# A graph layer's score rows: transposed on TensorE for each block, or stored in DRAM and fetched broadcast

## The chip, the cores and the metric

The kernel runs on one core of a Trainium2 chip. The metric is the device time of one execution in microseconds (us); less is better. Three executions of the kernel before took 2270.28, 2272.42 and 2273.19 us; the median, 2272.42, is the time before. The profile is of one execution more.

## The reference, cut to what matters

Two graph layers run over the same 3327 nodes. Layer 0 adds a normalised neighbour sum and a top-p attention, two steps each, to the features (256 wide). Layer 1, where the change lies, is graph attention with 4 heads of 64 features:

```python
h  = relu(layernorm(x))
hp = (h @ W).reshape(n, 4, 64)
s, d = einsum(hp, a_src), einsum(hp, a_dst)          # one score per head and node
e  = leaky_relu(s[:, :, None] + d[:, None, :], 0.2)  # head, row i, neighbour j
e  = where(adj > 0, e, -inf)
attn = softmax(e, axis=2)
x  = x + elu(einsum('hij,jhf->ihf', attn, hp))
```

The kernel uses that exp(leaky_relu(s+d)) is the larger of exp(s+d) and exp(0.2(s+d)). Up to a factor that belongs to row i alone, and so cancels in the softmax, that is qd[j] = exp(d[j]) times the larger of exp(0.8 s[i]) and low[j] = exp(-0.8 d[j]). The exp(0.8 s[i]) of a block's rows i, for each head, standing equal in all 128 partitions, are what the kernel calls both. A partition is a neighbour j.

## The kernel before

The nodes are padded to NP = 3328 = 26 tiles of 128. `fast` builds a list of some thousand pieces with `plan.put`: an engine, an estimated length, a rank, what must be done before (needs), and named buffers taken and given back. `Plan.order` (L497) plays this list against the estimated times, each engine taking the ready piece of the lowest rank, and the instructions are issued in that order. Nothing is reordered later: each engine works through its own queue, and the DMAs of nearly all pieces stand in the queue of SP. So a change of the list can also move pieces that it doesn't name.

Layer 0 (its second step is the stage before layer 1) works row tile by row tile. For a tile, TensorE makes 128 x 3327 logits (L845, from qq and kt), ScalarE their exponentials and counts (L856, L893, the latter writing to a scratch tile junk), VectorE the search for the top-p threshold and the cut (L948 to L1003), TensorE turns the kept weights (L1016, ScalarE copying, L1021) and multiplies them by the features (L1028). Beside it, `full` multiplies the adjacency by the features: L1049 loads up to four 128 x 128 tiles into one of four buffers at, L1060 multiplies, with the buffer c as the moving operand in step 1, L1067 and L1082 take the sum away. `finish2` (L1251) then does the tile's LayerNorms, its projection (L1289, L1298) and writes the tile's scores: sd (L1308, s and d of four heads), qd and low (L1303, L1304), and hp times qd into main (L1309).

Layer 1 is `attend_neighbours` (L1440). It has four blocks b of W = 832 output rows. Each block goes over the 26 neighbour tiles j:

- SP loads the block's adjacency for tile j into two at buffers (L1513); ScalarE makes a mask of 0 and 1 from it, in bfloat16 in a buffer et (L1523, L1524, two parts each).
- VectorE makes 4 x 832 exponents (L1535): larger of both and low, times mask. They go to one of four buffers e, or, for two tiles in six, to the two halves of rhs, which are free after layer 0 ("e2").
- TensorE multiplies them by main (L1551, into the two PSUM tiles pl) and, after each third tile, by qd for the denominators of three tiles (L1565, acca and accf).

At a block's end ScalarE copies the sums out of PSUM into one e buffer (L1605, L1608), TensorE turns them (L1626), VectorE inverts (L1630), ScalarE does the ELU's two functions (L1638), VectorE adds (L1642, L1643), and SP stores (L1646).

The row factors both are made by `broadcast` (L1463). For each of the 7 tiles that a block touches, four transposes of a score column spread over 128 columns (L1473) leave the row in all partitions in PSUM, and ScalarE's exponential (L1477) writes it into a half of the buffer c; the halves alternate between blocks. They need the tile's scores and `opened` (L1460): c is in use until all neighbour sums of layer 0 are added. Block b+1's pieces have a rank in the middle of block b, and need the end of block b-1, which used the same half.

Of the kernel before, what the change touches and what calls it, by code (L numbers as in the profile page):

```python
# [10 lines left out]
F32 = mybir.dt.float32  # L11
# [559 lines left out]
def fast(  # L571
# [33 lines left out]
    sd = const.tile([P, 2, NT, H], F32, name="sd")  # L605
    qd = const.tile([P, NT, H], F32, name="qd")
    low = const.tile([P, NT, H], F32, name="low")

    far = const.tile([P, 2], F32, name="far")
    bad = const.tile([P, STEPS, NT], F32, name="bad")  # L610
# [15 lines left out]
    with ExitStack() as l0:  # L626
# [184 lines left out]
            a = plan.put("ACT", 0.6, rank, exps, needs=[a])  # L811
            return plan.put("DVE", 0.6, rank, rest, needs=[a])

        plan = Plan(dict(pl=2, px=2, acca=1, accf=1, accf0=1, accf1=1, et=3, at=4, y=1, e2=2, mask=2, **BUFS))

        class Row:

# [532 lines left out]
        def search(row, rank, keys, stats_of, fresh):  # L1350
# [26 lines left out]
                ]  # L1377
                a = plan.put("POOL", (3.8, 4.7)[j], rank - (2.0, 1.6)[j], row.step, j, GP, needs=[got, more])
            if EVALS[n] == 3:
                a = plan.put("ACT", 3.05, rank - 1.4, row.count, 2, AF.Sign, needs=[a])  # L1380
                a = plan.put("DVE", 2.7, rank - 1.3, row.step, 2, V, needs=[a])
            halves = []
            for h in range(2):
# [56 lines left out]
        def attend_neighbours(rows, ends, done, fulls):  # L1440
# [2 lines left out]
            W = NP // 4  # L1443
            C = W // 2
            JG = 3
            logits_done = rows[-1].pieces["logits"]
            freed = [p for p in done]
            extra = {}

# [2 lines left out]
                return [both_of[:, k * NP : (k + 1) * NP].rearrange("p (h w) -> p h w", h=H) for k in range(2)]  # L1452

            def open_heads():
                extra["both"] = halves_of("c", None)

            def open_more():
                extra["e"] = halves_of("rhs", None)

            opened = plan.put("SP", 0.02, 59.0, open_heads, needs=[fulls], lag=0.0)  # L1460
            more = plan.put("SP", 0.02, 59.0, open_more, needs=[freed], lag=0.0)

            def broadcast(b, rank):  # L1463

                lo, hi = b * W, (b + 1) * W
                got = []
                for t in range(lo // P, -(-hi // P)):
                    held = {}

                    def turn(t=t, held=held):  # L1470
                        held["pb"] = ps_x.tile([P, H, P], F32, name="px")
                        for k in range(H):
                            T.transpose(held["pb"][:, k, :], sd[:, 0, t, k : k + 1].to_broadcast([P, P]), ident)  # L1473

                    def exps(t=t, held=held):
                        x0, x1 = max(lo, t * P), min(hi, t * P + P)
                        S.activation(  # L1477
                            extra["both"][b % 2][:, :, x0 - lo : x1 - lo],
                            held["pb"][:, :, x0 - t * P : x1 - t * P],
                            AF.Exp,  # L1480
                            scale=1.0 - ALPHA,
                        )

                    a = plan.put("PE", 0.55, rank, turn, needs=[ends[t][0], opened, used_heads[b % 2]], take=["px"])
                    got.append(plan.put("ACT", 0.65, rank, exps, needs=[a], give=["px"]))
                return got

            used_heads = [None, None]
# [2 lines left out]
            for b in range(4):  # L1491
# [14 lines left out]
                for j in range(NT):  # L1506
                    rank = r0 + 9.0 * j / NT
                    held = {}

                    def load(g, j=j, held=held, tiles=tiles):  # L1510
                        ts = tiles[4 * g : 4 * g + 4]
                        at = held[g] = apool.tile([P, 4, P], F32, name="at")
                        nc.sync.dma_start(  # L1513
                            at[:, : len(ts), :], adjt[ts[0] : ts[0] + len(ts), :, j, :].rearrange("i p q -> p i q")
                        )
# [9 lines left out]

                    def exponents(a, j=j, held=held, b=b):
                        if a == 0:
                            k = j % 6
                            held["e"] = (
                                epool.tile([P, NP], F32, name="e").rearrange("p (h w) -> p h w", h=H)  # L1530
                                if k < 4
                                else extra["e"][k - 4]
                            )
                        for k in (2 * a, 2 * a + 1):
                            V.scalar_tensor_tensor(  # L1535
                                held["e"][:, k, :],
                                extra["both"][b % 2][:, k, :],
                                low[:, j, k : k + 1],
                                held["mask"],
                                ALU.max,  # L1540
                                ALU.mult,
                            )
# [16 lines left out]
                    def sums(j=j, held=held, q=q, open_den=open_den):  # L1559
# [11 lines left out]
                                    tile_position=(0, 32 * k),  # L1571
                                )

                    loads = [
                        plan.put("SP", 0.1, rank, load, g, needs=[logits_done], take=["at"], lag=4.0) for g in range(2)
                    ]
                    m_ = plan.put("ACT", 2.2, rank, mask, needs=[loads], take=["et", "mask"], give=["at", "at"])
                    mine = "e" if j % 6 < 4 else "e2"
                    x_ = plan.put(
                        "DVE", 2.1, rank, exponents, 0, needs=[m_, both, ends[j][0], more if mine == "e2" else None,  # L1580
                        logits_done, last_e], take=[mine], hold=2.0,
                    )
                    y_ = plan.put("DVE", 2.1, rank, exponents, 1, needs=[x_], give=["et", "mask"], hold=2.0)
                    last_e = y_
                    x_ = plan.put(
                        "PE", 1.42, rank, product, 0, needs=[x_, last_acc, evacuated], take=["pl", "pl"] * (j == 0)
# [196 lines left out]
```

## Time and profile before

| What | Value |
|---|---|
| median of three executions | 2272.42 us |
| the profiled execution: time; span of its trace | 2271.77; 2269.9 us |
| ScalarE, GpSimd busy | 1480.0 (65%), 915.3 us (40%) |
| products L1551 into pl, from e and from rhs | 1664 matmuls of 128 x 416 |
| exponents L1535 | 416 of 128 x 832 |
| row exponentials L1477 | 28, median 590 ns |
| mask operations L1523, L1524 | 208 each, 112.1 and 114.5 us |
| loads at, 256 KB | 416, 2.7 us to landing in the median |
| HBM read over the span | 157.66 MB |

Each float32 matmul of the code appears as two in the profile, each transpose as one. PE is TensorE's matmul stream, PEld its weight loads, DVE VectorE, ACT ScalarE, POOL GpSimd, SP the engine whose queue issues the DMAs (SPq). The time of one record includes its way through the engine; what an engine gets through per time is seen from the distance of the starts. The profile's waits name who released an engine last. Layer 1 takes from about 1757 us to the end of the span, 2269.9.

### The profile page before, as it was taken

Reading aid. Unit: us, or ns where it says so; the run is one execution under the profiler, and the core shown is the slowest. Engines: PE = TensorE matmul, PEld = TensorE weight load, DVE = VectorE, ACT = ScalarE, POOL = GpSimd, SP = SyncE. Lnnn points to the kernel's source line nnn. Section 1 sums busy time; section 2 is a strip of 40 time slices with the busy share of each in tenths; the row PEclk is TensorE's granted clock in tenths of the full one; section 3 lists DMA queues with packets and bytes.
Section 4 is the critical chain, followed back from the end, with each engine's and each line's share of the span. In section 5 each row is a group of like instructions: output and inputs, shape, how many; then the busy total and the mean of one; then the engine's idle time right before and its main releaser. Section 6 shows DMA issues by size and latency. Waiting matters only on the chain. (4 is left out here: it accounts for less than half of the span.)

```text
span 2269.9 us, 36125 instructions
## 1 busy us (share of the span) xinstructions
PE 2207.6 (97%) x11956; PEld 1547.5 (68%) x11956; DVE 1618.2 (71%) x4273; ACT 1480.0 (65%) x2849; POOL 915.3 (40%) x2263
## 2 busy tenths in 40 slices
PE   7999999999999999999999999999999999999997
PEld 5477778777877778877878777878788433343332
DVE  5576656557565562277878898678776898989895
ACT  5766686677666851478887877777872646565553
POOL 6455555546533540256646656665561000000000
PEclk9999999999999999999999999999999999999998
DMA  3011221212212222531222122222222443434341
GB/s 98 20 37 53 83 69 53 64 51 61 74 48 74 69 82 76 183 86 54 65 57 73 56 61 70 70 75 75 67 74 78 119 118 107 120 106 120 102 126 42
DMA packets 189653, 176.96 MB, mean 78 GB/s; under 512 B 14866, under 2 KB 145808, under 8 KB 189328
## 3 DMA queue, kind: packets, MB, share of 16 engines
q1 hardware_dynamic: 187472, 173.30, 26.3%
q8 instruction: 96, 1.57, 0.3%
q10 hardware_dynamic: 1984, 1.26, 0.2%
q14 instruction: 101, 0.83, 0.1%
HBM read 157.66 MB, written 15.89 MB: 76 GB/s over the span
## 5 line engine op out<-in xcount | busy, mean ns | idle before, releaser
L1028 PE MATMUL acca<-rhs,et 128*128 128x256 f32 x2704 | 621.2, 380 | 0.8 <-ACT et L1021 0.8
L893 ACT ACTIVATE junk<-e,sc 128x3327 fp8e5<-128x3327 f32 x182 | 559.1, 3072 | 59.1 <-POOL sc L938 57.8
L1028 PEld LDWEIGHTS acca<-rhs,et 128*128 128x128 f32 x2704 | 498.5, 190 | 63.8 <-ACT et L1021 2.6
L1060 PE MATMUL accf<-main,at 128*128 128x257 f32 x1352 | 314.0, 382 | 4.9 <-DMA at<-in_adjt_dram 4.6
L1060 PE MATMUL accf<-c,at 128*128 128x256 f32 x1352 | 313.4, 382 | 4.8 <-ACT f L1067 4.7
L1535 DVE SCALAR_TENSOR_TENSOR e<-c,low,et 128x832 f32<-128x832 f32 x288 | 289.0, 1076 | 16.3 <-ACT e L1605 9.7
L1060 PEld LDWEIGHTS accf<-c,at 128*128 128x128 f32 x1352 | 250.2, 190 | 54.8 <-issue 14.1
L1060 PEld LDWEIGHTS accf<-main,at 128*128 128x128 f32 x1352 | 250.7, 191 | 47.1 <-issue 8.2
L1021 ACT COPY et<-px 128x512 f32<-128x512 f32 (+1 forms) x364 | 193.6, 553 | 133.3 <-PE acca L1028 72.5
L948 DVE SCALAR_TENSOR_TENSOR y<-e,sc 128x1664 f32<-128x1664 f32 x104 | 206.6, 1987 | 96.3 <-POOL sc L935 63.8
L953 DVE MAX8 cands<-y 128x8 f32<-128x208 f32 x832 | 242.7, 361 | 3.7
L1003 DVE SCALAR_TENSOR_TENSOR e<-e,thr 128x832 f32<-128x832 f32 x208 | 212.6, 1080 | 1.7
L1551 PE MATMUL pl<-e,main 128*64 128x416 f32 x1152 | 212.0, 516 | 0.1
L856 ACT ACTIVATE e<-pl 128x1024 f32<-128x1024 f32 x208 | 179.1, 863 | 45.6 <-PE pl L845 45.3
L1016 PE MATMUL px<-ident,e 128*128 128x128 f32 x1352 | 193.5, 275 | 7.6 <-ACT et L1021 4.5
L1524 ACT ACTIVATE et<-at 128x512 bf16<-128x512 f32 (+1 forms) x208 | 114.5, 550 | 127.6 <-DVE e L1535 82.4
L1016 PEld LDWEIGHTS px<-ident,e 128*128 128x128 f32 x1352 | 160.4, 141 | 51.6 <-issue 12.5
L845 PE MATMUL pl<-kt,qq 64*128 64x512 f32 (+1 forms) x728 | 184.1, 588 | 0.1
L1551 PEld LDWEIGHTS pl<-e,main 128*64 128x64 f32 x1152 | 79.8, 137 | 122.2 <-issue 102.2
L1535 DVE SCALAR_TENSOR_TENSOR rhs<-c,low,et 128x832 f32<-128x832 f32 x128 | 129.2, 1073 | 0.0
L845 PEld LDWEIGHTS pl<-kt,qq 64*128 64x128 f32 x728 | 70.9, 185 | 82.3 <-issue 76.5
L1523 ACT ACTIVATE at<-at 128x512 f32<-128x512 f32 (+1 forms) x208 | 112.1, 539 | 4.3 <-DMA at<-in_adjt_dram 4.2
(486 smaller groups left out, 2834.3 us busy)
## 6 DMA issues: line engine op xcount, KB each, us to landing
at<-in_adjt_dram SPq DMA_DIRECT2D x416, 256.0 KB, 2.7
at<-in_adjt_dram SPq DMA_DIRECT2D x104, 192.0 KB, 3.0
at<-in_adjt_dram SPq DMA_DIRECT2D x52, 128.0 KB, 2.1
ys<-ystage SPq DMA_DIRECT2D x26, 256.0 KB, 2.2
rhs<-in_x_dram SPq DMA_DIRECT2D x26, 128.0 KB, 2.9
ystage<-in_x_dram SPq DMA_DIRECT2D x26, 128.0 KB, 2.0
base<-ys SPq DMA_DIRECT2D x26, 128.0 KB, 2.2
x1s<-ystage SPq DMA_DIRECT2D x26, 128.0 KB, 1.7
```

The costliest lines, as they stand in the source:

```text
L845: T.matmul(pl[:, r, :m], qq[half, self.i, :], kt[half, 512 * k : 512 * k + m], start=True, stop=True,)
L856: S.activation(self.e[:, 1024 * k : 1024 * k + pl.shape[1]], pl, AF.Exp, accum_out=(self.p0, self.p1, self.p2, self.p3)[k],)
L893: S.activation(junk[:, :N], self.e[:, :N], fn, bias=t, scale=-1.0, accum_out=dst, saturate=False)
L948: V.scalar_tensor_tensor(self.y[:, : hi - lo], self.e[:, lo:hi], self.up, self.e[:, lo:hi], ALU.is_lt, ALU.mult, accum_out=(self.h0, self. ...
L953: V.max(self.cands[:, o // PIECE, :], self.y[:, o - lo : min(o + PIECE, hi) - lo])
L1003: V.scalar_tensor_tensor(piece, piece, self.thr[:, o : o + 1], piece, ALU.is_gt, ALU.mult)
L1016: T.transpose(pt[:, k, :], self.e[:, j * P : (j + 1) * P], ident)
L1021: S.copy(self.et[g][:, :m, :], self.pt.pop(g)[:, :m, :])
L1028: T.matmul(self.acc, et[:, j - 4 * g, :], rhs[self.n][:, j, :], start=(j == 0), stop=(j == NT - 1))
L1060: T.matmul(self.acc[:, : self.w], self.at[j // JC][:, j % JC, :], self.src[:, j, : self.w], start=(j == 0), stop=(j == NT - 1),)
L1535: V.scalar_tensor_tensor(held["e"][:, k, :], extra["both"][b % 2][:, k, :], low[:, j, k : k + 1], held["mask"], ALU.max, ALU.mult,)
L1551: T.matmul(q["acc"][a][k * FH : (k + 1) * FH, c, :C], main[:, j, h * FH : (h + 1) * FH], held["e"][:, h, c * C : (c + 1) * C], start=(j == 0),
```

## The change

- **Score rows.** `spread_heads` replaces the transposes of `broadcast`. In four groups of tiles (0 to 6, 7 to 12, 13 to 19, 20 to 25) one transpose turns a group's scores of four heads (up to 28 columns) into rows, one exponential takes them to SBUF (at most 28 partitions x 128), and SP stores them tile by tile, 4 rows of 512 bytes, into `highs`, 4 x 3328 in DRAM. A group's pieces are ready as soon as its scores are; the rank is 30 plus its last tile, at most 59.
- **Broadcast.** `broadcast` is two DMAs for a block, two heads each: 2 x 832 values read for each of the 128 partitions. They need the groups stored, the buffer opened, and the block before the last ended. A block's first half of exponents needs the first DMA, its second half the second.
- **Buffers.** Blocks 0 and 2 have both in the space of qq, free when the logits of the last row are done; blocks 1 and 3 in the first half of c. The second half of c becomes a third "e2", so seven buffers take exponents in turn instead of six.
- **First two tiles.** In block 0, tiles 0 and 1 get their adjacency into the space of kt and their masks into that of junk, by loads and masks of their own (one Relu and one Sign over 832 columns); the other tiles load as before.

```diff
-        logits_done = rows[-1].pieces["logits"]
+        logits_done = [r.pieces["logits"] for r in rows]
...
             def open_heads():
-                extra["both"] = halves_of("c", None)
+                both = wpool.tile([P, NT, P], F32, name="qq").rearrange("p t d -> p (t d)")
+                extra["both"] = [both.rearrange("p (h w) -> p h w", h=H)]
+
+                extra["at"] = wpool.tile([P, 2 * W], F32, name="kt").rearrange("p (k w) -> p k w", k=2)
+                extra["m"] = scr.tile([P, NP // 2], BF16, name="junk").rearrange("p (k w) -> p k w", k=2)
+
+            def open_heads2():
+                both, e = halves_of("c", None)
+                extra["both"].append(both)
+                extra["e"] = [e]
 
             def open_more():
-                extra["e"] = halves_of("rhs", None)
+                extra["e"] += halves_of("rhs", None)
...
+                def turn():
+                    held["ps"] = ps_x.tile([(t1 - t0) * H, P], F32, name="px")
+                    T.transpose(held["ps"], sd[:, 0, t0:t1, :].rearrange("p t h -> p (t h)"), ident)
+
+                def exps():
+                    held["rows"] = small.tile([7 * H, P], F32, name="rows", bufs=1)[: (t1 - t0) * H]
+                    S.activation(held["rows"], held["ps"], AF.Exp, scale=1.0 - ALPHA)
+
+                def store():
+                    for t in range(t0, t1):
+                        nc.sync.dma_start(
+                            highs[:, t * P : (t + 1) * P], held["rows"][(t - t0) * H : (t - t0 + 1) * H, :]
+                        )
...
+            cuts = (0, 7, 13, 20, NT)
+            spread = [spread_heads(*cuts[k : k + 2]) for k in range(4)]
...
                 lo, hi = b * W, (b + 1) * W
-                got = []
-                for t in range(lo // P, -(-hi // P)):
...
-                        for k in range(H):
-                            T.transpose(held["pb"][:, k, :], sd[:, 0, t, k : k + 1].to_broadcast([P, P]), ident)
...
-                    a = plan.put("PE", 0.55, rank, turn, needs=[ends[t][0], opened, used_heads[b % 2]], take=["px"])
-                    got.append(plan.put("ACT", 0.65, rank, exps, needs=[a], give=["px"]))
+                got, after = [], [spread[: b + 1], opened[b % 2], used_heads[b % 2]]
+                for a in range(2):
+
+                    def fetch(a=a):
+                        nc.sync.dma_start(
+                            extra["both"][b % 2][:, 2 * a : 2 * a + 2, :],
+                            highs[2 * a : 2 * a + 2, lo:hi].partition_broadcast(P),
                         )
 
+                    got.append(plan.put("SP", 0.1, rank, fetch, needs=[after], lag=7.0 + 5.0 * a))
                 return got
...
+                    def load_first(j=j):
+                        for t0, t1, w in ((0, W // P, P), (W // P, W // P + 1, W % P)):
+                            nc.sync.dma_start(
+                                extra["at"][:, j, t0 * P : (t1 - 1) * P + w].rearrange("p (i q) -> p i q", q=w),
+                                adjt[t0:t1, :, j, :w].rearrange("i p q -> p i q"),
+                            )
+
+                    def mask_first(j=j, held=held):
+                        held["mask"] = extra["m"][:, j, :]
+                        S.activation(extra["at"][:, j, :], extra["at"][:, j, :], AF.Relu)
+                        S.activation(held["mask"], extra["at"][:, j, :], AF.Sign)
...
-                            k = j % 6
+                            k = j % 7
...
+                    own = ["et", "mask"]
+                    if b == 0 and j < 2:
+                        loads, own = plan.put("SP", 0.2, rank, load_first, needs=[opened[0]], lag=4.0), []
+                        m_ = plan.put("ACT", 1.8, rank, mask_first, needs=[loads])
```

## The prediction

> **What bounds the kernel now.** I read the shares of the page first, then the windows of the last stage, then the chain of waits, then the groups of the lines that the change touches.
>
> ```profile
> PE 2207.6 (97%) x11956; PEld 1547.5 (68%) x11956; DVE 1618.2 (71%) x4273; ACT 1480.0 (65%) x2849; POOL 915.3 (40%) x2263
> ...
> L1535 DVE SCALAR_TENSOR_TENSOR e<-c,low,et 128x832 f32<-128x832 f32 x288 | 289.0, 1076 | 16.3 <-ACT e L1605 9.7
> ```
>
> TensorE is busy for 97% of the span. A busy share alone proves little there, so I look at its pace in layer 1 (chain of waits: start, length, what):
>
> ```profile
> 1787.51 8.53 PE pl L1551 x48
> 1800.36 8.53 PE pl L1551 x48
> 1813.22 8.53 PE pl L1551 x48
> ```
>
> The x48 products of three neighbour tiles start every 12.86 us, so a tile takes 4.286 us on TensorE (products and the denominator sums of L1565), without a gap. VectorE's four exponents of a tile take 4 x 1.003 us (289.0/288) = 4.01 us: 0.28 us per tile less. TensorE is the bound of a steady block, VectorE close behind. The windows cut layer 1 at the last neighbour product of layer 0 (1757.0), the first product of tile 3 (1787.4), the three block borders and the last sum:
>
> ```profile
> 1757.00:1787.40 30.40, 25.18 (x159) 13.45 (x157) 22.60 (x33) 23.31 (x49) 1.85 (x5) 0.89 0.44 125
> 1787.40:1887.10 99.70, 99.70 (x748) 37.71 (x744) 94.78 (x99) 45.51 (x92) 0.00 (x0) 1.00 0.37 107
> 1887.10:2008.50 121.40, 121.19 (x882) 46.61 (x881) 110.06 (x126) 69.66 (x172) 0.00 (x0) 1.00 0.39 114
> 2008.50:2128.70 120.20, 120.20 (x875) 46.21 (x874) 109.24 (x125) 68.77 (x170) 0.00 (x0) 1.00 0.40 115
> 2128.70:2247.70 119.00, 118.41 (x857) 43.92 (x853) 101.91 (x117) 61.01 (x154) 0.00 (x0) 1.00 0.33 96
> ```
>
> Columns: stretch, length, busy PE, PEld, DVE, ACT, POOL, granted clock, DMA share, GB/s. The first stretch is the only one with idle TensorE and a lowered clock: the ramp. Its timeline shows why:
>
> ```profile
> 1760.23 1.50 PE L1473 MATMUL px<-ident,sd 128*128 128x128 f32 x8 [2.15 <-ACT c L1477]
> ...
> 1769.48 16.02 DVE L1535 SCALAR_TENSOR_TENSOR e<-c,low,et 128x832 f32<-128x832 f32 x16
> ...
> 1771.47 1.74 PE L1551 MATMUL pl<-e,main 128*64 128x416 f32 x8
> ```
>
> The score rows of block 0 can be made only after layer 0 has left the buffer c, so the first exponents start 12.5 us after TensorE's last work of layer 0, and TensorE meanwhile transposes rows and waits for ScalarE's copies. The transposes themselves (minimum, median, maximum ns; first and last start):
>
> ```profile
> L1473 PEld LDWEIGHTS px<-ident,sd x112: 133/137/231, 1756.8 to 2081.1; 128*128 128x128 f32 x112
> L1473 PE MATMUL px<-ident,sd x112: 272/273/473, 1757.0 to 2081.3; 128*128 128x128 f32 x112
> ```
>
> Eight in a row (1886.11 to 1887.13) take 1.02 us, so one costs the stream about 0.137 us, its weight load, and not the 273 ns of its record.
>
> **What the Trainium skill says.** (1) "Perfetto Trace Analysis", Identifying the Most-Contended Engine: matmul busy share is no good measure; find the gaps. Here the 12.86 us spacing is that check. (2) "TensorE: Matmul & The Clock Gate", Part 2: only weight loads move ahead, matmuls stay in program order. So a product that waits for VectorE holds all behind it; the trace shows nothing against this. (3) "DMA: Bandwidth & Descriptors", Queues, rings and completion order: SP's DMAs share one ring on each of 16 engines, consumed in order. The trace agrees. Around the 1472 KB load at 814.7 us (issues from 812 to 826: size, us to landing) the neighbour tiles land in 7.9 us, against 2.7 over the run:
>
> ```profile
> qq<-qqs SPq DMA_DIRECT2D x1, 1472.0 KB, 9.5
> at<-in_adjt_dram SPq DMA_DIRECT2D x3, 256.0 KB, 7.9
> ```
>
> (4) Same page, Rules for kernel authors: a DMA that reads what another wrote must wait for the first one's completion before it is issued. The new fetches so wait on SP's queue, in order with the neighbour loads.
>
> **The change, part by part.** For the order I use the instructions of the changed kernel as built.
>
> *Transposes removed.* 112 x 0.137 = 15.3 us of TensorE. Of these 56 lie in the ramp (7.7 us) and 56 in blocks 0 to 2, where nothing covers them. Added: 4 transposes of a whole group of tiles, 0.14 each (same row) = 0.6. Net -14.7.
>
> *Ramp.* The 30.4 us hold 12.9 for three tiles, 2.1 for the last row's transposes and projection, 7.7 for the 56 transposes, and 7.7 of waiting. In the changed order the first product follows the last neighbour product directly: the exponents of tiles 0 and 1 are made before, since block 0's rows come into qq and two masks into kt and junk, all free once the last row is searched. Let that end be T. Tiles 0 and 1 keep TensorE until T+5.7. ScalarE masks tile 2 after the last copy (T+0.4+2.2), VectorE gives its halves at T+4.7 and T+6.7, in time; then the sums to T+12.9. Tile 3 is ready at T+10.7, tile 4 at T+14.7, then the last row's LayerNorm (1.6) and tile 5 at T+20.4, where TensorE waits 0.6. Below that I can't go. Above: block 1's rows, two DMAs of 832 KB, are issued into c at about T+1, as soon as VectorE has read c, and the loads of tile 4 stand behind them in the ring. The step-1 keys (384, 352 and 1472 KB, landed 10.9 us after 813.3) give 207 GB/s, hence an estimate of 8.2 us; at the 300 GB/s that the DMA table reaches in single slices, 5.7. Tile 4 then lands at T+10 to 12, is masked at T+13 to 14, and costs 2 to 4 us. Waiting left: 0.5 to 8 (all of today's), I take 2.5: -5.2.
>
> *Blocks.* A block is 26 x 4.286 = 111.4, plus 21 output transposes (0.80 for the first six, 0.48 for each three, from the timeline: 3.2). With 28 and 20 row transposes (3.8, 2.7) blocks 1 and 2 leave 2.9 and 2.8 us of waiting, block 3 4.4: 10.2 in all, at the borders. Who VectorE waited for there (1880 to 1920: total, times, longest):
>
> ```profile
> DVE e L1535 <- PE accf L1565: 5.5, 2, 4.9
> ```
>
> It sat 4.9 us without a free e buffer and then ran behind. A seventh e buffer lets it go one tile (4.0 us) further, and ScalarE loses 28 exponentials of 0.59. Against this, blocks 2's and 3's fetches are issued at a border, when VectorE ends the block before; behind them stand loads from tile 3 on and the output stores whose buffers ScalarE waits for. Loaded and masked tiles last VectorE about 12 us, against 8.2 plus 2.7 plus a mask of 2.2. I take 8.5 left (bounds 4 and 14): -1.7.
>
> *End of layer 0.* The first six exponents (6.0 us) stand inside row 25's search and row 24's end on VectorE, two masks (estimate 1.8 each from the 512 and 320 wide ones) before rows' copies on ScalarE. Behind them are row 25's transposes, but 40 neighbour products (40 x 0.445, from 12 in 5.34 us, = 17.8) stand ahead of those on TensorE and cover it; before, 18 of them stood at the very end. If that cover fails TensorE waits by the rest. Also 26 stores of 512-byte rows enter SP's queue, about 0.43 us each (kq spreads), up to seven together before neighbour loads: 3.0 us, against four tiles loaded ahead, 7.1 us of products. A store waits for its exponential on ScalarE, and SP with it. The rest of step 1 is only reordered. I take +1.0 (bounds -1 and +4).
>
> *Free edits.* The whole-tile masks save 0.4 us of ScalarE twice, under TensorE's stream; the failing-over test moves only in order.
>
> Sum: -14.7 - 5.2 - 1.7 + 1.0 = -20.6 us. The profiled execution took 2271.77 (span 2269.9 and 1.87 around it), giving 2251.2; it lies 0.65 below the median of the runs, 2272.42, so 2251.5 stands for the median after.
>
> **The rivals.** A: as above, 2251.5, own range 2247 to 2256: 0.50. B: VectorE's extra buffer also ends most border waits (4 left), the ramp waits 0.5 and layer 0 ends unmoved: -14.7 - 7.2 - 6.2 = -28, so 2244: 0.20. For it: the 4.9 us wait for a buffer; against: elu work still sits in ScalarE's queue there. C: the c fetch and the early exponents eat the ramp's gain (0, and +4 at the end of layer 0; borders as now): -10.7, so 2262: 0.19. E: C with 5 to 10 us more lost, for instance SP held by stores in several rows of layer 0: no difference, 2270: 0.05. D, slower: 128 partitions read the same 3.3 KB rows, and if such a read runs at 60 GB/s the 1.7 MB take 28 us; each of three late fetches then outlasts the 12 us of tiles in hand by 16: +48 - 22, 2298: 0.06. It decides from about 85 GB/s (20 us per fetch). Against it: four loads at 227.0 to 228.5, of which 512 KB are broadcast, landed by 234.3 beside neighbour tiles, 768 KB in 7.3 us.
>
> **Numbers.** The range 2243 to 2263 takes A, B's middle and most of C. A measurement of this kernel tells about 0.2% (4.5 us) from no change; faster by more: A, B, C = 0.89; within: 0.05; slower: 0.06.
>
> **What would show it.** L1473 and L1477 gone, PE in layer 1 keeping 12.86 us per three tiles, no PE idle or clock drop after the last L1060, blocks 1 to 3 of 116 to 119 us. Wrong: SP's fetches landing after more than 10 us with neighbour tiles behind them, products ended by VectorE in tiles 4 to 8, or L1060 products waiting for loads in step 1.

## The result, and the profile after

The changed kernel takes 2257.81 us (median of four executions, 2255.93 to 2259.07) against 2271.69 us for the kernel before on the same chip: the ratio is 0.9938, with a 95% interval of 0.9921 to 0.9955. So it is 13.9 us faster. The forecast was 20.6 us faster, 2251.5, with a range of 2243 to 2263. The direction and the range hold, but the time lies outside the prediction's own range for its main case (2247 to 2256), and a third of the forecast gain did not come. The profiled execution took 2258.68 us, its span is 2256.9, 13.0 less than the span before.

I read the same views as for the kernel before. All lines of the code after the change lie lower in the file: L1535 is now L1575 (exponents), L1551 is L1591 (products), L1565 is L1605 (sums), L1060 is L1061 (neighbour sums), L1605 is L1651 (sums to an e buffer), L1626 is L1672 (output transposes), L1630 is L1676 (reciprocals). First the shares of the page and the groups of the exponents, which now come from qq or c:

```profile
PE 2196.9 (97%) x11848; PEld 1535.3 (68%) x11848; DVE 1617.5 (72%) x4273; ACT 1466.3 (65%) x2821; POOL 924.8 (41%) x2263
...
L1575 DVE SCALAR_TENSOR_TENSOR e<-c,low,et 128x832 f32<-128x832 f32 x128 | 128.6, 1075 | 8.0 <-PE accf L1605 4.8
...
L1575 DVE SCALAR_TENSOR_TENSOR e<-qq,low,et 128x832 f32<-128x832 f32 x120 | 120.4, 1076 | 2.6 <-ACT e L1651 2.0
```

TensorE has 108 instructions less (112 transposes out, 4 in), ScalarE 28 less, and TensorE's share is 97% as before. The share does not tell which stage gained. The chain of waits shows the pace of a steady block, x48 products again every 12.86 us:

```profile
1910.91 8.53 PE pl L1591 x48
...
1923.77 8.53 PE pl L1591 x48
...
1936.63 8.53 PE pl L1591 x48
```

The windows of layer 1 (columns as before: length, busy PE, PEld, DVE, ACT, POOL, granted clock, DMA share, GB/s), cut at the last neighbour product, tile 3 and the block borders:

```profile
1760.90:1773.70 12.80, 12.80 (x98) 4.76 (x98) 9.90 (x13) 6.33 (x13) 2.23 (x2) 1.00 0.77 243
1773.70:1877.50 103.80, 102.62 (x749) 38.17 (x745) 100.02 (x111) 53.70 (x110) 3.73 (x3) 1.00 0.46 133
1877.50:1996.70 119.20, 118.00 (x859) 43.82 (x855) 110.21 (x126) 64.72 (x162) 0.00 (x0) 1.00 0.45 130
1996.70:2115.50 118.80, 118.21 (x857) 44.09 (x853) 109.79 (x126) 66.22 (x164) 0.00 (x0) 1.00 0.40 116
2115.50:2234.40 118.90, 118.31 (x858) 44.13 (x854) 100.61 (x116) 60.29 (x152) 0.00 (x0) 1.00 0.33 97
```

The first stretch, 30.4 us with an idle TensorE and a clock of 0.89 before, is 12.8 us without idle time at full clock. The three later blocks are only a little shorter. The starts of the products in the two traces give the whole account (us; "tile 6" is where the third group of three tiles starts):

| Piece | before | after | change |
|---|---|---|---|
| start to the last neighbour product | 1757.21 | 1760.89 | +3.68 |
| from there to tile 6 of block 0 (the ramp) | 43.08 | 28.65 | -14.43 |
| tiles 6 to 23 of block 0 | 77.14 | 79.27 | +2.13 |
| tiles 24 and 25 of block 0 | 9.69 | 8.67 | -1.02 |
| block 1 | 121.39 | 119.18 | -2.21 |
| block 2 | 120.18 | 118.86 | -1.32 |
| block 3 | 119.10 | 118.93 | -0.17 |
| after the last sum | 22.09 | 22.44 | +0.35 |
| sum | | | -12.99 |

The 2.13 us are the last row's own transposes and projection, which stood in the ramp before, and the fourth group's transpose. So the ramp gives 12.3 us, close to the 12.9 of the forecast. The blocks give 4.7 (tiles 24 and 25 of block 0, and blocks 1 to 3) where 9.4 were forecast, and layer 0 ends 3.7 us later where 1.4 were forecast (1.0 and three transposes).

**Where the blocks' gain went.** From the border to tile 6, blocks 1 to 3 take 33.25, 33.05 and 33.22 us before and 33.37, 33.04 and 33.05 after. Twelve transposes stood in this piece of each of blocks 1 and 2 before; they are gone, a buffer has come, and no piece moved by more than 0.2 us. The timeline of TensorE in block 2, the kernel before:

```profile
2008.52 4.41 PE L1551 MATMUL pl<-e,main 128*64 128x416 f32 x24
...
2031.61 0.65 PE L1473 MATMUL px<-ident,sd 128*128 128x128 f32 x4
...
2034.46 1.09 PE L1473 MATMUL px<-ident,sd 128*128 128x128 f32 x8
...
2041.57 7.20 PE L1551 MATMUL pl<-e,main 128*64 128x416 f32 x40
```

and after:

```profile
1996.65 1.62 PE L1591 MATMUL pl<-e,main 128*64 128x416 f32 x8
...
2015.46 2.29 PE L1591 MATMUL pl<-c,main 128*64 128x416 f32 x8
...
2020.05 2.61 PE L1591 MATMUL pl<-rhs,main 128*64 128x416 f32 x8 [0.24 <-DVE rhs L1575]
2022.84 2.61 PE L1591 MATMUL pl<-rhs,main 128*64 128x416 f32 x8 [0.18 <-DVE rhs L1575]
...
2029.70 3.01 PE L1591 MATMUL pl<-rhs,main 128*64 128x416 f32 x16
```

Both reach tile 6 after 33.05 us. After the change, eight products of tiles 4 and 5 take 2.29 and 2.61 us where eight take 1.4 to 1.6 elsewhere: TensorE waits for VectorE between these products, and the merged lines hide the waits. VectorE's own timeline of the changed kernel, at the same border, tells why (brackets: idle before, and who ended it):

```profile
1985.39 8.06 DVE L1575 SCALAR_TENSOR_TENSOR e<-qq,low,et 128x832 f32<-128x832 f32 x8
1995.45 4.07 DVE L1575 SCALAR_TENSOR_TENSOR e<-qq,low,et 128x832 f32<-128x832 f32 x4 [2.01 <-ACT e L1651]
...
2003.08 0.43 DVE L1688 SCALAR_TENSOR_TENSOR ystage<-ystage 128x256 f32<-128x256 f32 x1 [3.39 <-ACT ystage L1684]
...
2006.73 0.18 DVE L1676 RECIPROCAL mv<-px 128x4 f32<-128x4 f32 x1 [2.77 <-PE px L1672]
...
2008.29 2.08 DVE L1575 SCALAR_TENSOR_TENSOR e<-qq,low,et 128x832 f32<-128x832 f32 x2 [0.60 <-PE accf L1605]
```

Tiles 0, 1 and 2 of the block are done at 1999.4; the exponents of tile 3 start at 2008.29, 8.9 us later and 11.64 us after the border. The idle time is put down to three names, but what the exponents themselves wait for is the last one, `PE accf L1605`, the sums of tile 0. Tiles 0 to 3 of every block take the four buffers e, one of which holds the finished block's output at this time, so tile 3 needs the buffer of tile 0, and its sums stand behind the products of three tiles. The buffers for tiles 4, 5 and 6 lie free all the while. In the kernel before it is the same: tile 3 starts again 11.64 us after the border, which lies at 2008.52:

```profile
2020.16 2.08 DVE L1535 SCALAR_TENSOR_TENSOR e<-c,low,et 128x832 f32<-128x832 f32 x2 [0.60 <-PE accf L1565]
```

### The profile page after: what moved, and what is told of

The parts are those of the page before. It is cut to its first block, busy times and chain, and to the rows that moved or that the text cites. A ratio compares the mean times of both kernels' runs of the same rounds, so it can differ in the third digit from the quotient of the medians.

```text
span 2256.9 us, 35921 instructions
## 1 busy us (share of the span) xinstructions
PE 2196.9 (97%) x11848; PEld 1535.3 (68%) x11848; DVE 1617.5 (72%) x4273; ACT 1466.3 (65%) x2821; POOL 924.8 (41%) x2263
## 3 DMA queue, kind: packets, MB, share of 16 engines
q10 hardware_dynamic: 1984, 1.26, 0.2%
## 5 line engine op out<-in xcount | busy, mean ns | idle before, releaser
L1061 PE MATMUL accf<-main,at 128*128 128x257 f32 x1352 | 315.0, 383 | 4.3 <-DMA at<-in_adjt_dram 4.0
L1061 PE MATMUL accf<-c,at 128*128 128x256 f32 x1352 | 313.5, 382 | 5.1 <-ACT f L1068 4.5
L1061 PEld LDWEIGHTS accf<-c,at 128*128 128x128 f32 x1352 | 250.2, 190 | 55.2 <-issue 13.7
L1061 PEld LDWEIGHTS accf<-main,at 128*128 128x128 f32 x1352 | 251.2, 191 | 46.6 <-issue 8.2
L1022 ACT COPY et<-px 128x512 f32<-128x512 f32 (+1 forms) x364 | 193.5, 553 | 134.0 <-PE acca L1029 70.6
L1564 ACT ACTIVATE et<-at 128x448 bf16<-128x448 f32 (+1 forms) x204 | 112.2, 550 | 134.6 <-DVE e L1575 81.0
L1017 PEld LDWEIGHTS px<-ident,e 128*128 128x128 f32 x1352 | 160.2, 141 | 53.6 <-issue 12.8
L1591 PE MATMUL pl<-e,main 128*64 128x416 f32 x1024 | 187.0, 515 | 0.0
L1591 PEld LDWEIGHTS pl<-e,main 128*64 128x64 f32 x1024 | 71.2, 137 | 107.8 <-issue 93.4
L1575 DVE SCALAR_TENSOR_TENSOR e<-c,low,et 128x832 f32<-128x832 f32 x128 | 128.6, 1075 | 8.0 <-PE accf L1605 4.8
L1575 DVE SCALAR_TENSOR_TENSOR e<-qq,low,et 128x832 f32<-128x832 f32 x120 | 120.4, 1076 | 2.6 <-ACT e L1651 2.0
L1563 ACT ACTIVATE at<-at 128x448 f32<-128x448 f32 (+1 forms) x204 | 109.8, 538 | 18.2 <-DMA at<-in_adjt_dram 17.9
```

What stands on the lines that cost most here:

```text
L1017: T.transpose(pt[:, k, :], self.e[:, j * P : (j + 1) * P], ident)
L1022: S.copy(self.et[g][:, :m, :], self.pt.pop(g)[:, :m, :])
L1061: T.matmul(self.acc[:, : self.w], self.at[j // JC][:, j % JC, :], self.src[:, j, : self.w], start=(j == 0), stop=(j == NT - 1),)
L1575: V.scalar_tensor_tensor(held["e"][:, k, :], extra["both"][b % 2][:, k, :], low[:, j, k : k + 1], held["mask"], ALU.max, ALU.mult,)
L1591: T.matmul(q["acc"][a][k * FH : (k + 1) * FH, c, :C], main[:, j, h * FH : (h + 1) * FH], held["e"][:, h, c * C : (c + 1) * C], start=(j == 0),
```

## The experiments

All twelve kernels derive from the changed kernel. "Below before" is the kernel's median under that of the kernel before on the same chip (2272.5 to 2273.4 us there); the changed kernel has 13.9. The pieces are those of the table above.

| Kernel | median us | below before | ratio, 95% interval | border to tile 6, blocks 1, 2, 3 |
|---|---|---|---|---|
| rows turned on TensorE again | 2272.32 | 1.1 | 0.9995, 0.9987 to 1.0003 | 33.84, 33.74, 33.60 |
| six buffers | 2258.31 | 15.1 | 0.9934, 0.9920 to 0.9947 | 33.21, 33.21, 33.22 |
| no own buffers for tiles 0, 1 | 2265.61 | 7.8 | 0.9964, 0.9951 to 0.9978 | 33.60, 33.04, 33.04 |
| turned order of buffers | 2254.97 | 18.5 | 0.9917, 0.9904 to 0.9931 | 29.47, 29.61, 29.61 |
| transposes at the border | 2258.17 | 14.3 | 0.9935, 0.9922 to 0.9949 | 33.51, 33.04, 33.04 |
| transposes in the block | 2264.11 | 8.4 | 0.9962, 0.9948 to 0.9975 | 33.37, 33.60, 33.60 |
| late fetch | 2255.57 | 16.9 | 0.9924, 0.9911 to 0.9938 | 33.37, 33.05, 33.05 |
| rhs first | 2246.50 | 26.0 | 0.9885, 0.9870 to 0.9900 | 29.47, 29.61, 29.61 |
| rhs first and late fetch | 2244.27 | 28.5 | 0.9878, 0.9861 to 0.9894 | 29.47, 29.61, 29.61 |
| the same, rows late | 2250.49 | 22.3 | 0.9903, 0.9886 to 0.9919 | 29.47, 29.61, 29.61 |
| fetches twice | 2258.51 | 14.0 | 0.9940, 0.9926 to 0.9953 | 33.37, 33.04, 33.04 |
| rhs first, late fetch, fetches twice | 2244.62 | 27.9 | 0.9878, 0.9863 to 0.9893 | 29.47, 29.61, 29.61 |

**1. The rows turned on TensorE again.**

```diff
-                        nc.sync.dma_start(
-                            extra["both"][b % 2][:, 2 * a : 2 * a + 2, :],
-                            highs[2 * a : 2 * a + 2, lo:hi].partition_broadcast(P),
-                        )
...
+                        for k in range(H):
+                            T.transpose(held["pb"][:, k, :], sd[:, 0, t, k : k + 1].to_broadcast([P, P]), ident)
```

> The changed kernel, but with its row factors turned on TensorE again (112 transposes and 28 exponentials, no DRAM rows, no fetches); the seven buffers, the space of qq for blocks 0 and 2 and the first two tiles' own buffers stay. Theory: at each of the two inner borders 12 transposes lie in the first six tiles, where TensorE waits for VectorE anyway, so 24 x 0.137 = 3.3 us of the 14.7 were never to be had, and the kernel comes out 8.5 to 11.5 us above the changed one (the fetch of block 1 in front of tile 4's loads also goes, worth up to 3): 2266 to 2269. Rival, the prediction's step (nothing covers the transposes in the blocks): the full 14.7, 2272.5. In the profile the theory expects six tiles after a border to take 33.0 to 33.4 us as in both kernels; the rival 34.7.

Measured: 2272.32, 1.1 us below the kernel before on the same chip, so 12.8 above the changed one. The theory's number missed. The rival's number, 2272.5, was met, but by luck: its six tiles of 34.7 us did not come. Blocks 1 to 3 take 122.14, 121.74 and 119.48 us, 6.4 more than in the changed kernel, of which only 1.7 lie ahead of tile 6; and block 3, which has no transposes, has a third of these (33.60 us instead of 33.05). The rest of the 12.8 I had not foreseen: the early start is gone too. TensorE's timeline at the end of layer 0:

```profile
1748.08 7.93 PE L1061 MATMUL accf<-c,at 128*128 128x256 f32 x36
1755.85 1.04 PE L1510 MATMUL px<-ident,sd 128*128 128x128 f32 x8
...
1768.67 1.62 PE L1602 MATMUL pl<-e,main 128*64 128x416 f32 x8
```

The turns of block 0 stand in TensorE's queue behind the last 36 neighbour products, and the first product follows 12.65 us after the last of these, against 14.27 in the kernel before and none in the changed one. With the buffers alone the change is worth nothing that these runs can tell. SP's queue was what let block 0's rows overtake TensorE's work.

**2. Six buffers.**

```diff
-                            k = j % 7
+                            k = j % 6
...
-                    mine = "e" if j % 7 < 4 else "e2"
+                    mine = "e" if j % 6 < 4 else "e2"
```

> The changed kernel with six exponent buffers in turn as before (the second half of c unused). Theory: the seventh buffer bought nothing at the borders, because tile 3 of a block always waits for a buffer e that the sums of the block's tile 0 free: blocks 1 to 3 stay at 118.9 to 119.2 us each within 0.5, and only the ramp may lose up to 3 us, since tile 4 now needs a half of rhs: 2257.8 to 2261. Rival, the prediction's step (one buffer lets VectorE go a tile, 4.0 us, further at a border): blocks 1 to 3 become 2 to 4 us longer each, 2264 to 2270.

Measured: 2258.31, blocks of 119.03, 119.02 and 119.10 us against 119.18, 118.86 and 118.93, and the ramp's second group of three tiles 16.2 us against 15.9. The theory holds: the seventh buffer bought nothing at a border.

**3. No own buffers for the first two tiles.**

```diff
-                    if b == 0 and j < 2:
+                    if False:
```

> The changed kernel without the first two tiles' own buffers: their loads and masks use the common buffers at and et, rows still through DRAM. Theory: the loads then compete with layer 0's last neighbour loads and the masks with its last turned weights, so the first product comes 3 to 8 us after the last neighbour product instead of at once: 2261 to 2266. Rival (block 0's rows in qq alone make the early start): within 1 us of the changed kernel, 2257 to 2259.

Measured: 2265.61, 6.1 us less gain than the changed kernel. VectorE gets to the first exponents only after the last row's work, and TensorE shows the gap:

```profile
1766.40 13.37 PE L1591 MATMUL pl<-e,main 128*64 128x416 f32 x48 [6.06 <-DVE e L1575]
```

So the early start needs both parts: rows that come by DMA, and places for two tiles' masks. This kernel also answers a question on layer 0, taken up below.

**4. Another order of the same buffers.**

```diff
-                            k = j % 7
+                            k = (j + (0, 5, 4, 4)[b]) % 7
```

The line that names the buffer taken (`mine`) changes in the same way, here and in run 8.

> The changed kernel with the same seven buffers taken in another order: blocks 1 to 3 begin with the halves of rhs and c, free by then, instead of with the four e, of which a block's output takes one. Theory: VectorE's idle time at a border (2.0 us before tile 2, 8.9 before tile 3) goes, TensorE's waiting of 4.2 to 4.5 us per border falls to 0.5 to 1.5, blocks 1 to 3 take 115.5 to 116.5 us and the kernel 2247 to 2250. Rival (a border is set by ScalarE's and VectorE's output work, or by loads behind the fetches in SP's queue): blocks of 118 to 119.5 us, 2256 to 2259.

Measured: 2254.97, between the theory and the rival. At the border the theory is right: 29.5 and 29.6 us to tile 6 instead of 33.0 to 33.4, in all three blocks. Block 1 keeps it (115.28 us). In blocks 2 and 3 it is given back at once: tiles 6 to 8 take 16.78 us instead of 12.86, and the blocks 119.34 and 119.41. VectorE's timeline of block 2:

```profile
2013.02 0.42 DVE L1689 SCALAR_TENSOR_TENSOR ystage<-ystage,f 128x256 f32<-128x256 f32 x1
2017.41 0.18 DVE L1676 RECIPROCAL mv<-px 64x4 f32<-64x4 f32 x1 [3.96 <-PE px L1672]
2017.51 2.04 DVE L1575 SCALAR_TENSOR_TENSOR e<-qq,low,et 128x832 f32<-128x832 f32 x2
```

A reciprocal of 0.18 us stands in VectorE's queue ahead of tile 6's exponents and waits 3.96 us for the last output transpose. I took this wait for the reciprocal's, and run 8 was built on that. But the exponents of tile 6 could hardly have started sooner without it. In this order blocks 2 and 3 begin with the three "e2", so tiles 3 to 6 all want a buffer e, and one of the four still holds the output. Tile 6 must wait until the sums of tile 3 or the last output transpose give one back. TensorE's timeline of the same block:

```profile
2015.32 0.91 PE L1605 MATMUL acca<-e,qd 128*32 128x416 f32 x8
2016.04 0.88 PE L1605 MATMUL accf<-e,qd 128*32 128x416 f32 x8
2016.85 0.52 PE L1672 MATMUL px<-ident,e 128*64 128x128 f32 x3
```

The sums of tile 3 end at 2016.92 and the transpose at 2017.37; tile 6 starts at 2017.51. The reciprocal's place in the queue can explain 0.6 us of it at most. The rest is the wait that stood before tile 3, moved to tile 6: sums that stand behind the products of three tiles.

**5 and 6. The same 36 transposes at two places.** Their results are not read.

```diff
+                    if b and j in (3, 4, 5):
...
+                            for k in range(H):
+                                T.transpose(pb[:, k, :], sd[:, 0, j, k : k + 1].to_broadcast([P, P]), ident)
...
+                        plan.put("PE", 0.55, rank, again_turn, needs=[x_], take=["px"], give=["px"])
```

For the second, (12, 13, 14).

> The changed kernel with 12 transposes of score columns added back in each of blocks 1 to 3, four between the products of tiles 3, 4 and 5 each, their results read by nobody: 36 x 0.137 = 4.9 us of TensorE, just where VectorE paces it after a border. Theory: TensorE waits there anyway, so they cost 0 to 2 us in all (first six tiles of a block 33.0 to 33.7 us): 2258 to 2260. Rival, the prediction's step (nothing covers them): 2262.7, six tiles 34.7 us.

> The same 36 transposes, but at tiles 12, 13 and 14 of blocks 1 to 3, where TensorE is the bound. Theory and rival agree here on the full 4.9 us (2262 to 2263.5), with one group of three tiles of 14.5 us instead of 12.86 in each block; if it is clearly less, then TensorE has slack inside a block too and 0.137 us is too high a price.

Measured: at the border, 2258.17, with blocks of 119.32, 118.85 and 118.92 us: nothing. In the block, 2264.11, 0.6 above the forecast range, with blocks of 121.23, 121.46 and 121.53. The group of tiles 12 to 14 grows by 2.04 us (14.90 instead of the 14.5 expected), which is 0.170 per transpose: 0.145 from start to start, as the next lines show (0.58 for four), and the rest at each change of work, where the sixteen products ahead of the transposes take 2.95 us from start to start instead of 2.84.

```profile
1935.27 3.01 PE L1591 MATMUL pl<-rhs,main 128*64 128x416 f32 x16
1938.22 0.65 PE L1640 MATMUL px<-ident,sd 128*128 128x128 f32 x4
1938.80 3.02 PE L1591 MATMUL pl<-rhs,main 128*64 128x416 f32 x16
```

This is the clearest run of the study: the same instructions are free within six tiles of a border and cost more than their price ten tiles later. (The second kernel also loses 0.6 us ahead of tile 6 in blocks 2 and 3; why, I have not traced. Run 1 shows the same 33.60 in block 3.)

**7. Block 1's fetch held back** until block 0's loads of tile 8 have been issued and have landed.

```diff
-                got, after = [], [spread[: b + 1], opened[b % 2], used_heads[b % 2]]
+                got, after = [], [spread[: b + 1], opened[b % 2], used_heads[b % 2], late_after[:1] if b == 1 else None]
...
-            used_heads = [None, None]
+            used_heads, late_after = [None, None], []
...
+                    if b == 0 and j == 8:
+                        late_after.append(loads)
```

> The changed kernel with block 1's two fetches held back until block 0's loads of tile 8 are there, so that the loads of tiles 3 to 8 stand ahead of them in SP's queue. Theory: the second group of three tiles of block 0 takes 12.9 to 13.6 us instead of 15.9 (the three us of waiting in the ramp were the fetch in front of tile 4's loads): 2254.5 to 2256. Rival (the waiting comes from ScalarE's masks and the last row's work on VectorE): 15 to 16 us and 2257 to 2259.

Measured: 2255.57; the second group of three tiles takes 13.28 us instead of 15.86. ScalarE's timeline of the changed kernel, the masks of tile 4:

```profile
1765.37 0.47 ACT L1564 ACTIVATE et<-at 128x320 bf16<-128x320 f32 x1
1771.75 0.63 ACT L1563 ACTIVATE at<-at 128x512 f32<-128x512 f32 x1 [5.91 <-DMA at<-in_adjt_dram]
```

and with the fetch held back:

```profile
1764.59 0.47 ACT L1564 ACTIVATE et<-at 128x320 bf16<-128x320 f32 x1
1764.97 0.63 ACT L1563 ACTIVATE at<-at 128x512 f32<-128x512 f32 x1
```

The wait of 5.91 us for tile 4's load is gone. The ramp's wait was the fetch, as the prediction had it.

**8. rhs first.** The same as run 4 but with one shift for the three blocks. This moves the last reciprocal behind the exponents of tile 6. It also gives tile 6 the buffer c, and the fourth demand for a buffer e comes from tile 5, which can have that of tile 2, whose sums stand in the block's first group.

```diff
-                            k = j % 7
+                            k = (j + (0, 5, 5, 5)[b]) % 7
```

> The changed kernel with the seven buffers taken so that each of blocks 1 to 3 begins with the two halves of rhs, then the four e, then c. It differs from the earlier turned order only in blocks 2 and 3, where VectorE's last reciprocal now stands after the exponents of tile 6 and not before them. Theory: that reciprocal, 4 us of waiting with exponents behind it, was what gave blocks 2 and 3 their time back at tiles 6 to 8, so now all three blocks take 115 to 116 us: 2247 to 2249. Rival (loads behind the fetches or ScalarE's output work set tiles 6 to 8): blocks 2 and 3 stay at 118.5 to 119.5 us, 2254 to 2256.

Measured: 2246.50, just below the forecast, with blocks of 115.28, 115.42 and 115.49 us as forecast. The windows show a TensorE without idle time in all three:

```profile
1876.00:1991.30 115.30, 115.30 (x857) 43.42 (x853) 109.31 (x125) 64.70 (x162) 0.00 (x0) 1.00 0.46 134
1991.30:2106.70 115.40, 115.40 (x857) 43.42 (x853) 110.02 (x126) 66.20 (x164) 0.00 (x0) 1.00 0.42 119
2106.70:2222.20 115.50, 115.50 (x858) 43.44 (x854) 98.93 (x114) 60.41 (x152) 0.00 (x0) 1.00 0.34 99
```

The rival is out. But the number came right by luck as far as the reciprocal goes: two things changed at once, and the trace of run 4 speaks for the buffer. No run here moves the reciprocal alone. The three shifts give 12 us, and need no buffer, no instruction and no transfer more than the changed kernel has.

**9. Both repairs.** The edits of runs 7 and 8 together.

> The changed kernel with both repairs: blocks 1 to 3 begin with the halves of rhs, and block 1's fetches wait for the loads of tile 8. Theory: the two act at different places and add up, 11 us from the borders and 2.5 from the ramp: 2244 (2243 to 2245), first six tiles of block 0 in 26.0 to 26.5 us. Rival (with the ramp shortened, VectorE is later at block 1's border): 2246 to 2247.

Measured: 2244.27, 28.5 below the kernel before; block 0 reaches tile 6 in 26.14 us, blocks 1 to 3 are as in run 8. The two add up. This is the best version of the study, 1.2% below the kernel before.

**10. The same with the score rows late.**

```diff
-                a = plan.put("PE", 0.12, rank, turn, needs=[z[0] for z in ends[t0:t1]], take=["px"])
+                a = plan.put("PE", 0.12, rank, turn, needs=[z[0] for z in ends[t0:t1]] + [logits_done[:24]], take=["px"])
```

> The same with the first three groups of score rows transposed and stored only after the logits of layer 0's row 23, instead of row by row from 1226 us on, so that layer 0 keeps its former order up to there. Theory: layer 0 ended 1 to 3.7 us later in the profiles of the changed kernels than in that of the kernel before (1757.2 us), because the early transposes and 20 stores push its order about; then this ends at 1757 to 1758 us and the kernel comes out 1 to 2 us below the one with both repairs. Rival: the difference is scatter between executions (the streams are 1.3 us apart already at 1227 us, ahead of the first difference in order): no difference beyond 0.7 us.

Measured: 2250.49, 6 us worse than run 9, and neither expectation holds; the last neighbour product ends at 1767.77. The waits from 1690 us on name the reason:

```profile
ACT kt L1547 <- DMA kt<-in_adjt_dram: 6.1, 1, 6.1
...
PE px L1017 <- ACT et L1022: 5.6, 1, 5.6
```

The new order puts the first tiles' masks (L1547) on ScalarE ahead of the copies of a row's turned weights (L1022). The masks wait 6.1 us for the load into kt, which stands in SP's queue behind the fetch of block 0 and three neighbour loads, and TensorE waits 5.6 us behind the copies. It is what the prediction feared of the early masks, in an order where their cover is gone. On the question that the run was made for it says nothing.

**11 and 12. Fetches twice,** in the changed kernel and in the best one.

```diff
+                    def again_fetch(a=a):
+                        nc.sync.dma_start(extra["at"], highs[2 * a : 2 * a + 2, lo:hi].partition_broadcast(P))
+
+                    if b > 1 and a == 0:
+                        plan.put("SP", 0.1, rank, again_fetch, needs=[after])
...
+                    if b > 1 and a == 1:
+                        plan.put("SP", 0.1, rank, again_fetch, needs=[after])
```

> The changed kernel with the fetches of blocks 2 and 3 doubled: two more DMAs of 832 KB each time, into the space of kt, which nobody reads by then, one ahead and one behind the two real ones. So about 10 us more of transfers stand ahead of block 1's and block 2's first neighbour loads in SP's queue. Theory: at these borders VectorE stands idle until 11.6 us after the border, for want of a buffer e, and that covers most of it: blocks 1 and 2 grow by 0 to 2 us each, 2258 to 2262. Rival (a late fetch is paid for, as the prediction's slower case has it): 5 to 10 us more for each of the two borders, 2268 to 2278.

> The same doubled fetches in the kernel with both repairs (2244.3), where VectorE no longer stands idle at a border. Theory: now the cover is gone and the doubled fetch shows: 3 to 8 us more in each of blocks 1 and 2, 2250 to 2260. Rival (tiles in hand cover it here too): 2244 to 2247.

Measured: 2258.51 and 2244.62; the blocks are the same to 0.02 us as without the second fetches. The theory's number holds for the first and falls for the second, and with it falls the reason given for the first: the fetch is free at a border even where VectorE no longer idles for want of a buffer. SP's timeline of the second kernel shows it:

```profile
1855.05 0.48 SPq L1514 DMA_DIRECT2D kt<-highs  x1
1858.97 2.35 SPq L1508 DMA_DIRECT2D qq<-highs  x2
1861.92 0.36 SPq L1514 DMA_DIRECT2D kt<-highs  x1
1862.38 15.07 SPq L1560 DMA_DIRECT2D at<-in_adjt_dram  x8
```

The border of this kernel is at 1874.11. The two real fetches (L1508) are issued at 1858.97, when VectorE has ended the block, 15 us ahead of TensorE, and all four have moved their last packet at 1870.1. They lie in the time in which TensorE works off the buffers that VectorE has filled.

## Why the prediction was right in direction and too hopeful in size

- *Transposes removed, -14.7, "56 in blocks 0 to 2, where nothing covers them".* This step failed for 24 of the 56. They stood in the first six tiles of blocks 1 and 2, where VectorE sets the pace. Shown by the equal 33.05 us in both kernels and by runs 5 and 6. At 0.137 each this is 3.3 us of forecast gain that was not there. The other 32 in the blocks gave 4.7 us (1.02, 2.33 and 1.31 us in blocks 0, 1 and 2), 0.146 each. The price was a little off: 0.137 is the median weight load, while the eight in a row that the prediction shows give 1.02 / 8 = 0.13, and run 6 shows 0.170 among products.
- *Ramp, -5.2 beside the 7.7 of its transposes.* Right: 12.3 us of 12.9. The waiting left was taken at 2.5 and is 3.0 (15.86 us for tiles 3 to 5 instead of 12.86), and its mechanism, the fetch into c ahead of tile 4's loads, is shown by run 7, which leaves 0.4. Tile 4's load kept ScalarE until T+10.9 and its mask was done at T+13.0; the forecast had T+10 to 12 and T+13 to 14.
- *Blocks, -1.7, "A seventh e buffer lets it go one tile (4.0 us) further".* This failed. I counted the buffers and not which tile takes which. Counted from the border, VectorE starts tile 2 only 0.4 us earlier in blocks 1 and 2 and 1.4 in block 3 (its idle time there fell from 4.9 to 2.0 us mostly because tiles 0 and 1 came later), and then stands before tile 3 until 11.6 us after the border, as before. The line that the step was read from holds two waits: 4.9 us before tile 2 and only the last 0.6 before tile 3. The rest of the stand before tile 3 has other names in the profile, output transposes and ScalarE, and I passed over it. Run 2 shows the seventh buffer to be worth nothing in that order, runs 4 and 8 that the order is worth 12 us. "Perfetto Trace Analysis", Optimization Strategy, says that a gap that repeats can mean too few buffers for the next tile to be allocated. It points at the right place here, the 8.9 us between tiles 2 and 3 at a border, but the count was not what was short: three free buffers lay beside the gap. The argument against, fetches and loads in SP's queue, falls too (runs 11 and 12).
- *End of layer 0, +1.0 (-1 to +4).* In the profile +3.7; with three of the new transposes 1.4 were forecast. The instructions are the same in both kernels up to the first early transpose, at 1222.7 us in the changed one, and by then it is already 1.4 us late. (The expectation of run 10 puts the first difference after 1227 us; that is wrong.) My mark, close behind, is the copy that ends the eighth row's attention. In the fourteen profiles it starts between 1222.7 and 1225.9. From it to the last neighbour product the kernel before takes 533.4 us, the changed one 535.8, and nine others with the same rows (runs 2, 4 to 9, 11 and 12) 535.2 to 535.7. Without the early masks and exponents (run 3) it is 535.6, without the rows (run 1) 533.3. So the real cost is about 2.1 us. It is not the early exponents, which the prediction feared here; their cover holds. It comes with the three early transposes (0.4), the 20 stores and the order that they bring about. How it divides among these stays open, since run 10 lost more elsewhere.
- *Rivals.* The outcome lies between A and C, and the stated range holds it because it takes in most of C, not because the blocks did what A says. C's reason, that the fetch and the early exponents eat the ramp's gain, is not what happened. D is excluded: the packets of a pair of fetches (3328 bytes each, 512 of them, 1.7 MB) run from first to last in 7.0 to 7.6 us in the changed kernel, 223 to 242 GB/s beside neighbour loads. My estimate was 8.2; D needed 20.
- *What would show it.* L1473 and L1477 are gone, the 12.86 us stand, TensorE is not idle and its clock does not fall at the start of layer 1, and the blocks (119.2, 118.9, 118.9) lie at the upper end of the 116 to 119 us. That end was the sign: the border had not moved. And one sign of being wrong did show: products of tiles 4 and 5 of a block are ended by VectorE.

In the sum, 7.6 us are missing between the two profiles (6.7 between the medians): 4.7 in the blocks, 2.3 at the end of layer 0, of which 1.4 were there before the kernels differ, about 0.6 in the ramp, 0.35 after the last sum, less 0.3 of rounding and of the fourth transpose.

## What to carry to other kernels

Work taken off the busiest engine pays only where this engine sets the pace. Compare the length of the same piece, such as border to tile 6, with and without the work, before multiplying a count by a price. At a seam between two stages ask which buffer the first late tile takes and what releases it: the order in which buffers go round can matter more than their number. And when the profile puts a long wait down to a short instruction, ask when the work behind it could have started at the earliest: in run 4 that left 0.6 us of 3.96.

## What the runs showed of the hardware that was not expected

- With two more fetches at a border, four pairs of heads, 3.4 MB in packets of 3328 bytes, went in 13.5 to 14.1 us, and the DMA engines moved up to 418 GB/s in a slice of 1.25 us, all partitions reading the same rows of DRAM. In the slices of 418 GB/s all packets were theirs. No sign of a penalty for the same address was seen.
- GpSimd's small operations became slower beside the early exponents: the first after each LayerNorm's variance took 0.96 us beside them (median over the run 0.227), the second 1.25 (median 0.569). The timeline of GpSimd in the changed kernel, while VectorE runs four exponents from 1742.46 on:

```profile
1742.64 0.96 POOL L673 TENSOR_SCALAR mv<-mv 128x1 f32<-128x1 f32 x1 [6.22 <-DVE mv L668]
1743.69 1.25 POOL L674 TENSOR_TENSOR mv<-mv,powers 128x1 f32<-128x1 f32 x1
```

  "SBUF — State Buffer", SBUF: two separate sides, says that VectorE and GpSimd share a port pair, which a VectorE operation with two SBUF inputs holds against a GpSimd operation that reads SBUF, for the whole instruction. The exponents have two such inputs and take 1.0 us each; the trace agrees. In run 3, without the early exponents, the same operations of the row before the last took 0.22 to 0.28 and 0.56 to 0.57 us; those that fell beside exponents there, a little later, took 0.96 and 1.26.
- Executions of one and the same instruction stream were 3.2 us apart after some 1225 us (kernel before, runs 1 and 10: 1223.8, 1222.7 and 1225.9), while run 10 keeps the distances of the kernel before to 0.3 us from there to 1601, as long as the two have the same order. A shift of 1 or 2 us at a late mark of one profile is no finding; the distance between two marks, 533.3 and 533.4 against 535.2 to 535.8, was.
